# Two edge components in one 64-column matmul, in both layers of a graph network, and a reordered prologue

## The chip, the cores and the metric

The kernel runs on one core of a Trainium2 chip. The metric is the device time of one execution in microseconds (us), taken as the median over a number of runs. The engines are called PE (TensorE matmuls; PEld is its weight loads), DVE (VectorE), ACT (ScalarE), POOL (GpSimd) and SP (SyncE, which here issues DMAs).

## The reference

Two layers of an equivariant graph network follow each other, each as `x = layernorm(x + layer(x))`. There are 6,250 nodes and 200,000 edges, sorted by destination. A node has 64 scalars and 32 vectors of three components, 160 numbers in all. A layer does this:

```
h     = node_linear(x)                      # scalars 64x64, vectors 32x32, times a node attribute
w     = silu(edge_scalars @ W1) @ W2        # 10 -> 100 -> 192 in layer 1, 64 -> 64 -> 224 in layer 2
e0,e1 = edge_attr[:, :1], edge_attr[:, 1:4] # one scalar and one 3-vector for each edge
mid   = products of w, h[src] and e0/e1     # scalar, dot, outer, vector (layer 2: also the cross product)
agg   = segment_sum(mid, dst) / 4           # sum over the edges that end at a node
out   = self part of x + node_linear(agg)   # layer 2 ends with silu and sigmoid gates
```

## The kernel before, in words

**Edges.** 200,000 edges are 1,563 tiles of 128. Four tiles are a unit, so a layer has 391 units; two tiles are a pair. Consecutive tiles form groups of 3 to 12 (284 groups), such that the destinations of a group fit a window of 32 nodes. A check at run time (`flag`) makes sure of that; with other data a general branch (`general`) would run, which does not run here.

**A unit of a layer** (function `windows`) is spread over a software pipeline written by hand: `gather` (four units ahead) fetches the rows `h[src]` from DRAM with indirect DMAs on POOL, two per pair; `hidden` (three ahead) is the first edge matmul with its silu on ACT; `weights` and, on DVE, `places` and `products` are two ahead. `places` makes for each tile four matrices of 128 edges by 32 window positions: one-hot rows times the edge attribute component c = 0..3 (tile `sel`). `products` makes `mid`, the products of weights and gathered rows, in four instructions a pair in layer 1 and six in layer 2. `aggregate` then sums the edges of a tile on PE:

```python
for c, (at, step, k) in enumerate(sums):
    ...
    matmul(pg[32 * c:32 * c + 32, :k * V], s[:n, t % 2, c, :], o,
           start=first, stop=last, tile_position=(0, 32 * c))
```

That is four matmuls a tile, one for each edge component. Each has 32 weight columns at its own place of the array (0, 32, 64, 96) and writes its own 32 partitions of the accumulator `pg`. It streams k x 32 columns of `mid`: 5, 3, 3 and 3 blocks in layer 1, and 5, 5, 5, 5 in layer 2. PE's instructions are kept in program order.

**End of a group.** ACT copies `pg` to `r` (in layer 2 also the last 32 columns, block by block, to `rest`: L772). One unit later, `turn` transposes `r` on PE, and DVE adds it at the group's window into the node sums `sm` (four blocks) and `sr` (L788, L790).

**Nodes.** When a block of 128 nodes has all its edges, `second_nodes` or `last_nodes` multiplies its sums by the output weights (`rm0`, `rr0`, `rm1`, `rr1`), adds the self part and normalises; these steps are slipped in between units, one at a time.

**Prologue.** All node blocks are loaded, transposed (`turn_nodes`) and multiplied (`send_nodes`), and the result is stored to DRAM for the gathers, four blocks at a time and the short last block at the end. After the sixth of these steps DVE runs the check (`check`: 11 subtractions over 128 x 1,563 numbers, three reductions). After the last store, the products of layer 1's output weights are formed on PE and copied by DVE into `rm0` and `rr0` (L389 to L397), and the first gather follows.

The order across engines is that of the instructions in the program and of the buffers: eight buffers of gathered rows (`g`), three of weights (`pw`), six of `sel` and of `mid`, two of `pg`.

Of the kernel before, what the change touches and what calls it, by code (L numbers as in the profile page):

```python
# [86 lines left out]
def kernel(ctx: ExitStack, tc: tile.TileContext, a, out):  # L87
# [34 lines left out]
    SLOTS = (448, 640)  # L122
# [25 lines left out]
    chunks = [range(b, min(b + BG, NB - 1)) for b in range(0, NB - 1, BG)] + [range(NB - 1, NB)]  # L148
# [12 lines left out]
    def spread(t, s, v, n, q):  # L161

        nc.vector.memset(t, 0.0)
        q.dma_start(t[0:S, 0:n], a[s])
        for k in range(2):
            q.dma_start(t[S + k * V:S + k * V + V, n + k * V:n + k * V + V], a[v])
# [3 lines left out]
    spread(l1[:, 0], "Ws_l1_a", "Wv_l1_a", S, nc.scalar)  # L170
    spread(l1[:, 1], "Ws_l1_c", "Wv_l1_c", S, nc.scalar)
    ident = const.tile([P, P], F32, name="ident")
    make_identity(nc, ident)
    for j, (k, q) in enumerate((("a", nc.scalar), ("c", nc.gpsimd))):
        for r in range(0, P, V):
            q.dma_start(l1z[r:r + V, j, :], a[f"Wv_l1_{k}"])
# [47 lines left out]
    rm0 = const.tile([96, 4, 2, S + V], F32, name="rm0")  # L224
    rr0 = const.tile([64, 2, 2 * V], F32, name="rr0")
# [4 lines left out]

    limits = pre.tile([1, 2, NG], F32, name="limits")
    nc.gpsimd.memset(limits[:, 0], 0.0)
    for b, g in enumerate(READY):
        if g < NG:
            nc.gpsimd.memset(limits[:, 0, g:min(READY[b + 1], NG)], float(P * (b + 1)))
    g0 = 0
    while g0 < NG:
        g1 = g0
        while g1 < NG and zeroed(g1) == zeroed(g0):
            g1 += 1  # L240
        nc.gpsimd.memset(limits[:, 1, g0:g1], float(zeroed(g0) - W))
        g0 = g1

# [4 lines left out]
    def turn_nodes(bs, x):  # L248
# [12 lines left out]
        if (bs[0] // BG) % 2:  # L261
            nc.scalar.activation(xt[:, :w], p[:, :w], AF.Copy)
        else:
            nc.vector.tensor_copy(xt[:, :w], p[:, :w])
# [3 lines left out]
    def send_nodes(bs, xt, zt):  # L268
# [13 lines left out]
        for j, (b, q) in enumerate(zip(bs, qs)):  # L282
            t = rows[:n, j, :]
            nc.scalar.activation(t, q[:, 0, :], AF.Copy, scale=nv[:n, b, 0:1])
            nc.vector.scalar_tensor_tensor(t, q[:, 1, :], nv[:n, b, 1:2], t,
                                           op0=OP.mult, op1=OP.add)
# [14 lines left out]

    def check():

        basef = pre.tile([1, NG], F32, name="basef")
        nc.vector.tensor_copy(basef, base)
        nc.vector.tensor_copy(off, raw)
        p = psum.tile([P, 512], F32, name="pw", bufs=3)
        matmul(p[:, :NG], ones, basef, start=True, stop=True)
        for g0, g1 in segments:
# [3 lines left out]
            nc.vector.tensor_tensor(o, o, p[:, g0:g1, None].to_broadcast([P, m, n]), OP.subtract)  # L313

        nc.vector.memset(off[tail_e:, NT - 1:], 0.0)
        ends = pre.tile([P, 2], F32, name="ends")
        nc.vector.tensor_reduce(ends[:, 0:1], off, AX.X, OP.max)
        nc.vector.tensor_reduce(ends[:, 1:2], off, AX.X, OP.min)

        nc.vector.tensor_scalar(ends[:, 0:1], ends[:, 0:1], float(W - 1), None, op0=OP.subtract)  # L320
        nc.vector.scalar_tensor_tensor(over, ends[:, 1:2], -1.0, ends[:, 0:1],
                                       op0=OP.mult, op1=OP.max)

        nc.vector.tensor_tensor(limits[:, 0], limits[:, 0], basef, OP.subtract)
        nc.vector.tensor_tensor(limits[:, 1], basef, limits[:, 1], OP.subtract)
        nc.vector.tensor_reduce(tops[:, 1:2], limits, AX.XY, OP.max)

    def checked():
# [7 lines left out]
    previous = None  # L336
    for c, (bs, x) in enumerate(zip(chunks, xs)):
# [4 lines left out]
        if c == 5:  # L342
            check()
    send_nodes(previous[0], *previous[1])
    checked()


# [27 lines left out]

    p = psum.tile([P, 512], F32, name="pw", bufs=3)
    q = p[:96, :192].rearrange("p (j d) -> p j d", j=2)

    for j in range(2):
        for o, w, m in ((q[:, j, 0:S], w23[:, j * 96:j * 96 + 96], w23[:, 192:256]),
                        (q[:, j, S:], w23[:, 256 + j * 96:352 + j * 96], w23[:, 448:480])):
            matmul(o, w, m, start=True, stop=True)
        for k in range(2):
            matmul(p[k * V:k * V + V, 192 + j * V:224 + j * V],
                   w23[:, 320 + j * 96:352 + j * 96], w23[:, 448:480], start=True, stop=True,
                   tile_position=(0, k * V))
    nc.vector.tensor_copy(rm0[0:64, 0, :, 0:S], q[0:64, :, 0:S])  # L389
    nc.vector.tensor_copy(rm0[64:96, 0, :, S:], q[64:96, :, S:])  # L390

    for c, at_c, at_d in ((1, (32, 64), 0), (2, (0, 64), 32), (3, (0, 32), 64)):
        for k, r in enumerate(at_c):
            nc.vector.tensor_copy(rm0[r:r + 32, c, :, S:], q[32 * k:32 * k + 32, :, S:])
        nc.vector.tensor_copy(rm0[at_d:at_d + 32, c, :, 0:S], q[64:96, :, 0:S])
    for k in range(2):
        nc.vector.tensor_copy(  # L397
            rr0[k * V:k * V + V, :, k * V:k * V + V],
            p[k * V:k * V + V, 192:256].rearrange("p (j d) -> p j d", j=2))

# [6 lines left out]
    for at, n, f in ((0, 160, 0.125), (160, 32, r3 / 8), (192, 32, r2 / 8)):  # L407
# [8 lines left out]
            ((C0, vx), (F, vz), (C1, vx), (Dd, ss), (F, vy)),  # L416
            ((F, vz), (C0, vy), (C1, vy), (F, vx), (Dd, ss)),
            ((F, vy), (Dd, ss), (C0, vz), (F, vx), (C1, vz)))
# [7 lines left out]
    for o, f in ((rm1[:, :, 0:96], fs), (rm1[:, :, 96:], fv), (rr1[:, 0:96], fs),  # L426
                 (rr1[:, 96:], fv), (rm1[32:64, 1, vz], -1.0), (rm1[96:128, 2, vx], -1.0),
                 (rm1[0:32, 3, vy], -1.0)):
# [47 lines left out]
    def second_nodes(b, work, clear, name="nx"):  # L476
# [26 lines left out]
        def summed():  # L503
            p = psum.tile([P, 512], F32, name=bank[0], bufs=bank[1])
            q = p[:n, :2 * D].rearrange("p (w d) -> p w d", w=2)
            for c in range(4):
                l = sm[:96, c, rows]
# [6 lines left out]
            matmul(q[:, :, S + V:D], sr[:64, rows], rr0, start=False, stop=True)  # L514
# [25 lines left out]
    def last_nodes(b, work, clear):  # L540
# [19 lines left out]
        def summed():  # L560
# [5 lines left out]
            for c in (1, 2, 3):  # L566
                v = slice(96 if c == 2 else 0, 192)
# [26 lines left out]
    def windows(i, loads, work, inputs_of):  # L594
# [4 lines left out]
        scalar = lambda w, place: (w, V, 0, 2, place, 2)  # L599
        vector = lambda w, place, step, c=0, n=3: (w, 0, S + c * V, n, place, step)  # L600
        kinds = ((scalar(0, 2), scalar(S, 5), vector(128, 9, 2), vector(160, 0, 3)),
                 (scalar(0, 2), scalar(S, 10), vector(128, 9, 2), vector(160, 5, 3, 0, 2),
                  vector(160, 1, 1, 2, 1), vector(192, 0, 3)))[i]

        sums = (((5, 2, 5), (0, 2, 3), (2, 1, 3), (2, 2, 3)),
                ((9, 1, 5), (2, 1, 5), (0, 2, 5), (0, 1, 5)))[i]
# [144 lines left out]
        def aggregate(t):  # L751
# [6 lines left out]
            for c, (at, step, k) in enumerate(sums):  # L758
                o = mid[:n, t % 2, V * at:V * at + V]
                o = bass.AP(tensor=o.tensor, offset=o.offset, ap=[o.ap[0], [V * step, k], [1, V]])  # L760
                matmul(pg[32 * c:32 * c + 32, :k * V], s[:n, t % 2, c, :], o,
                       start=first, stop=last, tile_position=(0, 32 * c))
            if last:
                r = work.tile([P, 160], F32, name="r")
                w = (96, P)[i]
                nc.scalar.activation(r[:, :w], pg[:, :w], AF.Copy)  # L766
                if i == 0:
                    nc.scalar.activation(r[:32, 96:], pg[:32, 96:160], AF.Copy)
                else:
                    for c in range(4):  # L770
                        k = slice(32 * c, 32 * c + 32)
                        nc.scalar.activation(rest[g % 3][k, k], pg[k, P:P + V], AF.Copy)  # L772
                made["r", g] = r

        def turn(g):
            r = made["r", g]
            pt = pair[g % 2][:, 2 * P:]
            if i == 0:
                transpose(pt[:96, :P], r[:, :96], ident)
# [277 lines left out]
```

## Time and profile before

| what | value |
|---|---|
| median of 16 runs | 5844.52 us (5809.98 to 5873.43) |
| the profiled execution: time, span | 5881.2 us, 5879.4 us |
| mean granted TensorE clock | 0.758 |
| PE, DVE, POOL, ACT busy | 75%, 52%, 52%, 20% |
| first gather, first layer's last node step, end | 66.6 us, about 2945 us, 5879.4 us |

The profile is one execution. A line of it names the program's line, the engine, the operation and its tiles, written as result<-operands, with the number of instructions after an x. A group line goes on with busy time, the mean of one in ns, the idle time of the engine ahead of it, and what ended that. In a timeline line the first two numbers are the start and the length in us, and brackets hold idle time ahead of it with its releaser; "issue" means that the engine waited for nothing the profile shows. The clock row gives tenths of full TensorE speed. All matmuls of the main loop stand under L138, the line of a helper, and all transposes under L143, so tiles tell them apart: `pair<-e,fc` is `hidden`, `pw<-fc,h` is `weights`, `pg<-mid,sel` is `aggregate`, `pair<-ident,r` is `turn`, `pn` are node blocks.

### The profile page before, as it was taken

How to read it: one execution, taken by the hardware profiler on the slowest of the kernel's cores; microseconds unless marked ns; L12 is line 12 of the kernel's file. 1: busy time of each engine (PE TensorE's matmuls, PEld its weight loads, DVE VectorE, ACT ScalarE, POOL GpSimd, SP SyncE). 2: the span in 40 equal slices, each digit the busy share in tenths (PEclk: the TensorE clock that was granted, in tenths of full speed). 3: DMA queues.
4: the chain of work that ended last, by engine and by line, in shares of the span. 5: the costliest groups of instructions: out<-in, count | busy, mean ns of one | idle time of the engine just before them, and what ended most of it. 6: DMA issues, size and time to landing. Idle time of an engine off the chain costs nothing. (4 is left out here: it accounts for less than half of the span.)

```text
span 5879.4 us, 108061 instructions
## 1 busy us (share of the span) xinstructions
PE 4401.6 (75%) x37363; PEld 2847.1 (48%) x37363; DVE 3053.5 (52%) x13202; ACT 1172.6 (20%) x4012; POOL 3078.7 (52%) x3232
## 2 busy tenths in 40 slices
PE   7888877777777767777766777776777776677777
PEld 4555555555555545555534444444444444444554
DVE  5554444444445445444545555555555555555555
ACT  2111111111122212222211011111121222222333
POOL 4555555555555555554355555555555555544543
PEclk7787777777778777777767777777777777777777
DMA  3222222222222222222222222222222222222221
GB/s 101 59 62 58 59 55 56 55 53 56 55 55 55 54 55 56 53 55 53 52 65 67 68 69 69 70 68 68 68 69 66 68 66 65 66 62 65 67 66 44
DMA packets 298518, 364.06 MB, mean 62 GB/s; under 512 B 86324, under 2 KB 246205, under 8 KB 297965
## 3 DMA queue, kind: packets, MB, share of 16 engines
q0 software_dynamic: 151056, 257.36, 18.1%
q1 hardware_dynamic: 121740, 85.59, 5.6%
q10 hardware_dynamic: 25168, 14.11, 0.8%
q8 instruction: 301, 4.93, 0.3%
q14 instruction: 253, 2.06, 0.1%
HBM read 338.73 MB, written 18.03 MB: 61 GB/s over the span
## 5 line engine op out<-in xcount | busy, mean ns | idle before, releaser
L710 POOL DMA_INDIRECT g<-table,src x3126 | 3057.0, 978 | 2760.5 <-DVE mid L728 1538.2
L728 DVE TENSOR_TENSOR mid<-g,pw 128x128 f32<-128x128 f32 (+2 forms) x7820 | 1842.4, 298 | 458.1 <-remote 246.9
L138 PE MATMUL pg<-mid,sel 128*32 128x160 f32 (+1 forms) x25008 | 1600.1, 350 | 284.7 <-issue 281.3
L138 PE MATMUL pw<-fc,h 100*128 100x192 f32 (+1 forms) x6252 | 1463.1, 428 | 248.3 <-issue 189.6
L138 PEld LDWEIGHTS pw<-fc,h 100*128 100x128 f32 (+1 forms) x6252 | 1029.0, 231 | 734.0 <-issue 657.5
L138 PEld LDWEIGHTS pg<-mid,sel 128*32 128x32 f32 x25008 | 938.7, 132 | 685.0 <-issue 544.4
L741 DVE SCALAR_TENSOR_TENSOR sel<-iota,off,ea 128x128 f32<-128x128 f32 x3126 | 947.6, 341 | 594.2 <-remote 289.5
L788 DVE TENSOR_TENSOR sm<-pair,sm 96x128 f32 (+1 forms) x568 | 164.2, 289 | 1229.7 <-PE pair L143 386.2
L143 PE MATMUL pair<-ident,r 128*96 128x128 f32 (+1 forms) x852 | 262.9, 334 | 716.9 <-ACT h L672 339.1
L138 PE MATMUL pair<-e,fc 64*100 64x256 f32 (+1 forms) x2348 | 719.8, 517 | 59.7 <-issue 35.5
L143 PEld LDWEIGHTS pair<-ident,r 128*96 128x96 f32 (+1 forms) x852 | 124.6, 146 | 939.5 <-ACT h L672 373.4
L766 ACT ACTIVATE r<-pg 128x96 f32<-128x96 f32 (+1 forms) x568 | 149.3, 263 | 1917.1 <-remote 862.0
L138 PEld LDWEIGHTS pair<-e,fc 64*100 64x100 f32 (+1 forms) x2348 | 298.6, 212 | 302.6 <-issue 249.9
L672 ACT ACTIVATE h<-pair 100x256 f32<-100x256 f32 x782 | 259.0, 378 | 907.6 <-PE pair L138 324.3
L683 ACT ACTIVATE h<-pair 128x256 f32<-128x256 f32 x392 | 149.9, 383 | 961.9 <-remote 427.1
L138 PE MATMUL pn<-rm,sm 96*128 96x128 f32 (+3 forms) x968 | 193.7, 352 | 29.0 <-issue 26.0
L772 ACT ACTIVATE rest<-pg 32x32 f32<-32x32 f32 x1136 | 209.1, 184 | 12.6 <-issue 0.3
L138 PEld LDWEIGHTS pn<-rm,sm 96*128 96x128 f32 (+2 forms) x968 | 175.6, 234 | 46.6 <-issue 42.1
L138 PEld LDWEIGHTS pair<-fold,rest 128*128 128x128 f32 x568 | 132.6, 285 | 12.0 <-ACT rest L772 9.3
L143 PE MATMUL pn<-ident,nx 128*128 128x128 f32 (+1 forms) x242 | 66.6, 368 | 87.3 <-DVE nx L460 71.0
L517 DVE SCALAR_TENSOR_TENSOR nx<-pn,gets,nx 128x160 f32<-128x160 f32 x96 | 36.5, 380 | 171.8 <-PE pn L138 63.6
L440 ACT ACTIVATE xt<-pn 128x128 f32<-128x128 f32 (+1 forms) x146 | 40.4, 277 | 425.0 <-PE pw L138 200.8
(153 smaller groups left out, 1558.3 us busy)
## 6 DMA issues: line engine op xcount, KB each, us to landing
g<-table,src POOLq DMA_INDIRECT x3126
e<-in_e SPq DMA_DIRECT2D x781, 64.0 KB
e<-in_e SPq DMA_DIRECT2D x390, 20.0 KB
ea<-in_ea_main SPq DMA_DIRECT2D x63, 96.0 KB
xg<-in_x_main SPq DMA_DIRECT2D x12, 320.0 KB
table<-rg SPq DMA_DIRECT2D x12, 320.0 KB
xmid<-nx ACTq DMA_DIRECT2D x48, 80.0 KB
table<-nr ACTq DMA_DIRECT2D x48, 80.0 KB
```

The costliest lines, as they stand in the source:

```text
L138: r = nc.tensor.matmul(*args, **kw)
L143: r = nc.tensor.transpose(*args)
L440: nc.scalar.activation(xt[:, 0, :n], p[:, 0:n], AF.Copy)
L517: nc.vector.scalar_tensor_tensor(y, q[:, k, :], gets[:n, b, k:k + 1], y, op0=OP.mult, op1=OP.add)
L672: nc.scalar.activation(h[:100, 2 * P * j:2 * P * j + m], pair[j][:100, :m], AF.Silu)
L683: nc.scalar.activation(h[:kk, c0:c1], p[:kk, c0:c1], AF.Silu, scale=0.125)
L710: nc.gpsimd.indirect_dma_start(out=g[:n, j, :], out_offset=None, in_=table[i][:, :], in_offset=bass.IndirectOffsetOnAxis(ap=of(t)[0], axis=0))
L728: nc.vector.tensor_tensor(parts(mid[:n, :m], V * place, V * step, k), parts(g[:n, :m], c, V, k), parts(q[:n, :m], w, w_step, k), OP.mult)
L741: made["last"] = nc.vector.scalar_tensor_tensor(s[:n, j], iota[:n, None, :].to_broadcast([n, 4, W]), w, e[:, :, None].to_broadcast([n, 4, ...
L766: nc.scalar.activation(r[:, :w], pg[:, :w], AF.Copy)
L772: nc.scalar.activation(rest[g % 3][k, k], pg[k, P:P + V], AF.Copy)
L788: nc.vector.tensor_tensor(sm[:h, :, at], pt[:h, :P].rearrange("p (c w) -> p c w", c=4), sm[:h, :, at], OP.add)
```

## The change

A tile is aggregated with three matmuls instead of four: two of 32 weight columns and one of 64, which sums two edge components at once into 64 partitions.

- Layer 1: component 0 in 32 columns streams 5 blocks (160 columns), component 1 streams 4 blocks (128), components 2 and 3 together in 64 columns stream 4 blocks (128).
- Layer 2: component 0 and component 3 in 32 columns stream 5 blocks each (160), components 1 and 2 together in 64 columns stream 7 blocks (224).

A 64-column matmul gives both components all the blocks that either needs, so `mid` is laid out anew (`kinds`) and some sums are formed that are not used. In layer 1 the window sums now fill 128 partitions of `sm` and 32 of `sr`; the weights `rm0`, `rr0`, `rm1` and `rr1` follow, and a node block of layer 1 gets one more matmul. In layer 2 the end of a group has two more copies, since the used columns differ between partitions.

In the prologue the short block goes first. The check's conversions and subtractions move from DVE to POOL, its three reductions stay on DVE, each placed behind a block's last sum. The composed weights are formed in the middle, copied once by ACT, and placed by DVE three copies at a time. Eight DMAs that repeated a small weight become two. The general branch is adapted to the new layout.

```diff
-        sums = (((5, 2, 5), (0, 2, 3), (2, 1, 3), (2, 2, 3)),
-                ((9, 1, 5), (2, 1, 5), (0, 2, 5), (0, 1, 5)))[i]
+        sums = (((0, 1, 5, 1, 5), (1, 1, 0, 1, 4), (2, 2, 1, 1, 4)),
+                ((0, 1, 9, 1, 5), (3, 1, 0, 1, 5), (1, 2, 1, 1, 7)))[i]
...
-            for c, (at, step, k) in enumerate(sums):
+            for c, m, at, step, k in sums:
+                q = c if i == 0 else (0, 2, 3, 1)[c]
...
-                matmul(pg[32 * c:32 * c + 32, :k * V], s[:n, t % 2, c, :], o,
-                       start=first, stop=last, tile_position=(0, 32 * c))
+                matmul(pg[32 * q:32 * (q + m), :k * V],
+                       s[:n, t % 2, c:c + m, :].rearrange("p c w -> p (c w)"), o,
+                       start=first, stop=last, tile_position=(0, 32 * q))
...
-                    for c in range(4):
+                    nc.scalar.activation(r[64:96, :P], pg[64:96, V:V + P], AF.Copy)
+                    nc.scalar.activation(
+                        r[96:, :P].rearrange("p (h v) -> p h v", h=2),
+                        pg[96:, :192].rearrange("p (h v) -> p h v", h=2)[:, :, :2 * V], AF.Copy)
+                    for c, at in enumerate((P, P, P + V, P + 2 * V)):
...
-            matmul(q[:, :, S + V:D], sr[:64, rows], rr0, start=False, stop=True)
+            matmul(q[:, :, S + V:S + 2 * V], sm[:, 0, rows], rr0[:, 0], start=False, stop=False)
+            matmul(q[:, :, S + 2 * V:D], sr[:V, rows], rr0[:V, 1], start=False, stop=True)
...
-    chunks = [range(b, min(b + BG, NB - 1)) for b in range(0, NB - 1, BG)] + [range(NB - 1, NB)]
+    chunks = [range(NB - 1, NB)] + [range(b, min(b + BG, NB - 1)) for b in range(0, NB - 1, BG)]
...
-            nc.vector.tensor_tensor(o, o, p[:, g0:g1, None].to_broadcast([P, m, n]), OP.subtract)
+            nc.gpsimd.tensor_tensor(o, o, base_of[:, g0:g1, None].to_broadcast([P, m, n]),
+                                    OP.subtract)
...
+        if c == 3:
+            nc.gpsimd.tensor_copy(basef, base)
+            nc.gpsimd.tensor_copy(off, raw)
+        if c == 6:
+            bases()
+            check()
+        if c == 7:
+            small = composed()
+        if c > 7:
+            for step in small[:3]:
+                step()
+            small = small[3:]
+        if c > 8 and reduces:
+            with tc.issue_after(last[0].ins):
+                reduces.pop(0)()
```

## The prediction

> **What bounds the kernel now.** I read the page first: the span, the busy shares and the granted clock.
>
> ```profile
> span 5879.4 us, 108061 instructions
> ...
> PE 4401.6 (75%) x37363; PEld 2847.1 (48%) x37363; DVE 3053.5 (52%) x13202; ACT 1172.6 (20%) x4012; POOL 3078.7 (52%) x3232
> ...
> PEclk7787777777778777777767777777777777777777
> ```
>
> PE is the busiest engine, at a mean granted clock of 0.76. The busy time cut into prologue with first fill, layer 1 and layer 2 says how much slack each has:
>
> ```profile
> 105.00:2945.00 2840.00, 2209.72 (x18949) 1496.62 (x18948) 1398.91 (x5790) 540.76 (x1726) 1509.08 (x1537) 0.77 0.23 56
> 2945.00:5879.00 2934.00, 2123.91 (x18054) 1302.37 (x18054) 1596.89 (x7203) 604.94 (x2207) 1522.29 (x1563) 0.74 0.27 66
> ```
>
> Columns: window, its length, busy PE, PEld, DVE, ACT, POOL, then clock. PE idles 630 us in layer 1 and 810 us in layer 2; DVE and POOL are near half. What ends PE's idle time, from its waits:
>
> ```profile
> PE pair L143 <- ACT h L672: 339.1, 99, 7.3
> PE pair L143 <- ACT h L683: 291.5, 64, 8.7
> PE pg L138 <- issue: 281.3, 493, 2.5
> PE pw L138 <- issue: 189.6, 341, 2.4
> ```
>
> With the smaller rows, 578 us are "issue" (PE waits for nobody that the profile shows) and some 860 us are the rest, mostly the group's transpose waiting behind ACT. So PE's own work is most of a unit of four tiles, and the waits come on top. Then the timeline, around single bursts of the aggregation. First the weight loads, then PE:
>
> ```profile
> 1508.80 0.95 PEld L138 LDWEIGHTS pg<-mid,sel 128*32 128x32 f32 x32 [0.23 <-issue]
> 1510.00 0.31 PEld L138 LDWEIGHTS pair<-e,fc 64*100 64x100 f32 x3 [0.25 <-issue]
> ...
> 4420.96 0.97 PEld L138 LDWEIGHTS pg<-mid,sel 128*32 128x32 f32 x32
> 4422.18 0.30 PEld L138 LDWEIGHTS pair<-e,fc 128*128 128x128 f32 x2 [0.25 <-issue]
> ...
> 4443.75 1.80 PEld L138 LDWEIGHTS pg<-mid,sel 128*32 128x32 f32 x32
> 4446.04 0.50 PEld L138 LDWEIGHTS pair<-e,fc 128*128 128x128 f32 x2 [0.49 <-issue]
> ...
> 4010.52 0.73 PEld L138 LDWEIGHTS pg<-mid,sel 128*32 128x32 f32 x16
> 4011.74 0.50 PEld L138 LDWEIGHTS pair<-e,fc 128*128 128x128 f32 x2 [0.49 <-issue]
> ```
>
> ```profile
> 4000.26 0.75 PE L138 MATMUL pg<-mid,sel 128*32 128x160 f32 x16
> 4000.94 0.70 PE L138 MATMUL pair<-e,fc 128*128 128x256 f32 x2
> ```
>
> Each matmul leaves two records (two passes), so a unit's 16 matmuls are 32, and a round is one pass in each of the four places. Three readings. (1) A unit's burst takes 1.20 us in layer 1 (1508.80 to 1510.00) and 1.22 us in layer 2 (4420.96 to 4422.18), although layer 1 streams 160+96+96+96 columns a tile and layer 2 four times 160. The four places run side by side, and the widest, 160 in both layers, sets the time. (2) Eight rounds take 1.22 us and four 0.68 (4000.26 to 4000.94): a round costs 0.135 us and a burst 0.14 us once. At half clock (windows on these bursts give a clock of 1.00 and 0.50) it is 2.29 and 1.22: 0.267 and 0.15. (3) The once-only part sits at the change of shape: the weight loader idles 0.25 us (0.49 at half clock) before the first load of another shape, waiting for nobody, while its 32 loads of one shape have no such gap.
>
> **The change, part by part.**
>
> *Three matmuls a tile.* The built program has, per tile, 32 columns, 32 columns, 64 columns, then the next tile's 32: two changes of shape a tile. The trace shows many pairs of shapes among ordinary matmuls (rows 32, 64 or 128 against columns 32 or 128), and each has the gap; 32 against 64 columns at unlike places is not among them. Bounds: below, no gap, the three side by side; above, the gap each time. I take the upper one, because the gap comes with every pair of shapes that occurs, also where only rows or only columns differ.
>
> Then a tile is two bursts. The 32-column pair: two rounds at 160, 2 x 0.135 + 0.14 = 0.41 us. The 64-column one in layer 1: 128 columns, 2 x 0.108 + 0.14 = 0.36; in layer 2: 224 columns, 2 x 0.189 + 0.14 = 0.52. A unit: 4 x 0.77 = 3.06 us in layer 1 and 4 x 0.93 = 3.71 in layer 2, against 1.22: +1.84 and +2.49. At half clock 5.05 and 6.34 against 2.29: +2.76 and +4.05. The clock rows 0.77 and 0.74 mean 46% and 52% of the time at half speed: +2.26 and +3.30 a unit, times 391 units: 884 + 1290 = 2174 us of PE work.
>
> What hides it: PE's waits for others. They come as 99 waits of 3.4 us and 64 of 4.6 us; a unit that is 2.26 or 3.30 us longer swallows about 69% of each, of 860 us some 595. The issue gaps stay; matmul and weight-load records fall by 12,504 of 74,726, 17%, so I take 17% of 578 off: 98 us. Net 2174 - 595 - 98 = +1481. Bounds: all at full clock with every wait swallowed, (1.84 + 2.49) x 391 - 860 = +830; all at half clock with nothing swallowed +2660.
>
> [...]
>
> *Copies after a group.* Layer 2 gets two more ACT copies, 568 in all at 184 to 276 ns: 105 to 157 us of an engine that is 20% busy. PE reads them a unit later, so the unit hides them: 0, and at most 157 if not. Layer 1's copy goes from 250 to 276 ns: 0. DVE's sums over 96 or 128 partitions are 288 and 290 ns, its products keep their number: 0.
>
> *Node blocks.* One more matmul in each of 49 blocks: two records of 376 ns become two of about 282 (row 96x64) and two of about 355 (row 32x64), +0.5 us each, 0 to +25; taken +13.
>
> *Prologue.* The work before the edges ends on DVE:
>
> ```profile
> 66.62 1.04 POOL L710 DMA_INDIRECT g<-table,src  x1 [40.51 <-DVE rr L397]
> ...
> 38.54 1.22 PE L138 MATMUL pg<-l,xt 128*128 128x256 f32 x2 [6.07 <-DVE rg L285]
> ```
>
> The check held PE for 6.07 us, and the copies into rm and rr from 62.82 to 66.1 stand between the last store and the first gather. Both go: -9.4. Against it: the short block's load goes ahead on SP (0.66 us) and the last block sent is now a full one (about 1 us): -8. Queued on POOL instead: 11 subtractions of 1,563 columns. No POOL row shows such an operation; its memset of 768 columns took 0.76 us, its select of 128 took 0.33, so 1.6 to 4 us. POOL idles 40.5 us there and nothing else is queued behind but the gathers, which wait for DVE anyway; without that cover, +4. Eight l1z loads become two, ahead of nothing late: 0. The fallback branch is not run: 0.
>
> Sum: 1481 + 13 - 8 = +1486 on the profiled 5881 us, 7367; the median of the runs lies 37 us under that execution: **7330 us**.
>
> **Rivals.**
>
> *Side by side after all, slower by the widest* (16%). 32 and 64 columns overlap without a gap. Layer 1 keeps 160 as its widest and pays nothing; layer 2 goes to 224: a round 0.054 us longer, 0.107 at half clock, 0.65 a unit, 255 us, less 64 waits x 0.65 = 42, less 98 of issue, less 8: +107, so 5951. For it: the places are independent within one shape. Against: reading (3).
>
> *Faster through fewer instructions* (15%). As before, but layer 2's wider place is never last, because the unit's end is set by ACT's transposes and issue gaps. Then only -98 and -8 remain: 5738. It decides if layer 2's units are not longer by even 0.27 us on average, the point where 0.27 x 391 = 106 us uses the gain up. For it: the timeline's units vary from 3 to 14 us, so other things than the burst decide many. Against: no idle on PE long enough in most units.
>
> *No change to measure* (5%): the two cancel. That the change is not what it says is ruled out by the built program.
>
> **How the numbers follow.** The gap case has 64%: seen at every change of shape, unseen at this one. Its own range is 6750 to 8050, inside its bounds of 6674 and 8504. The rivals lie at 5951 and 5738. A range from 5780 to 8000 leaves out most of the faster case (12%) and the top of the gap case (7%). About 0.3% (18 us) is what a measurement of this kernel can tell from no change; faster by more has 15%, within 5%, slower by more 64 + 16 = 80%.
>
> **What would show it.** In the changed profile: bursts of pg with a unit at 3 to 6 us instead of 1.2 to 2.3; weight loads of 128x64 starting over 0.2 us after the matmul before them; PE busy over 85% and POOL's wait for DVE mid longer; the first gather near 58 us. A unit's burst near 1.2 us in layer 1 and 1.6 in layer 2, at full clock, would make the gap wrong; more than 17% less issue idle would favour the faster case. A granted clock far from 0.76 would move the size, not the sign.

## The result, and the profile after

The changed kernel takes 6068.97 us in the median (6046 to 6107), the kernel before 5849.37 us beside it: a ratio of 1.0385, 95% interval [1.0363, 1.0407]. The sign of the forecast holds and the time lies inside its range, but the size is wrong: +220 us came where +1486 were worked out. The profiled execution took 6054.6 us.

The page of the changed kernel, the rows that answer to those of before:

```profile
span 6052.8 us, 95930 instructions
...
PE 5297.5 (88%) x31205; PEld 2752.8 (45%) x31205; DVE 3048.8 (50%) x13185; ACT 1364.2 (23%) x4583; POOL 3128.1 (52%) x3248
...
PEclk8898898888897898888788898998999989989898
```

PE's busy time grew by 896 us and the span by 173 (the profiled execution of before was slower than its median, that of the changed kernel faster). The clock row, sevens before, is eights and nines: 0.879 in the mean instead of 0.758. By stage, with the same columns as before (layer 2 begins near 3000 us):

```profile
105.00:3000.00 2895.00, 2655.97 (x15935) 1505.86 (x15933) 1394.70 (x5784) 546.16 (x1730) 1528.33 (x1536) 0.86 0.22 54
3000.00:6052.00 3052.00, 2573.86 (x14912) 1200.34 (x14912) 1597.06 (x7203) 790.42 (x2770) 1542.71 (x1563) 0.90 0.25 63
```

PE idles 239 us in layer 1 (630 before) and 478 in layer 2 (810). Its waits:

```profile
PE pair L143 <- ACT h L712: 299.6, 97, 7.4
PE pair L143 <- ACT h L701: 144.2, 71, 5.6
...
PE pg L138 <- issue: 60.8, 104, 3.2
...
PE pw L138 <- issue: 14.9, 22, 2.2
```

The waits of the group's transposes for ACT's `h` fell from 631 to 444 us. The idle time at `pg` and `pw` that was put down to "issue" fell from 471 to 76. Now the timeline around two bursts in layer 2, weight loads of one first, then PE of the other (granted clock 1.00 in both):

```profile
4557.24 0.19 PEld L138 LDWEIGHTS pg<-mid,sel 128*64 128x64 f32 x2 [0.25 <-issue]
4557.76 0.14 PEld L138 LDWEIGHTS pg<-mid,sel 128*32 128x32 f32 x4 [0.33 <-issue]
4558.16 0.19 PEld L138 LDWEIGHTS pg<-mid,sel 128*64 128x64 f32 x2 [0.25 <-issue]
```

```profile
4580.53 3.74 PE L138 MATMUL pg<-mid,sel 128*32 128x160 f32 x24
```

The gap that the forecast assumed is there at every change between 32 and 64 columns inside the bursts (5270 in the trace, the weight loader idle for 0.12 us at the least, 0.25 or 0.33 us in the median, by direction), and a unit's burst in layer 2 at full clock takes 3.67 us until the next matmul starts (4580.53 to 4584.20; forecast 3.71). So the price of the edit was read rightly. What shrank is elsewhere. The groups of PE, before and then after (busy time, mean ns, idle time ahead):

```profile
L138 PE MATMUL pg<-mid,sel 128*32 128x160 f32 (+1 forms) x25008 | 1600.1, 350 | 284.7 <-issue 281.3 <-DVE mid L728 1.1
L138 PE MATMUL pw<-fc,h 100*128 100x192 f32 (+1 forms) x6252 | 1463.1, 428 | 248.3 <-issue 189.6 <-DVE mid L728 52.1 <-PE pw L138 0.9
```

```profile
L138 PE MATMUL pg<-mid,sel 128*32 128x160 f32 x18756 | 3065.4, 347 | 62.6 <-issue 60.8 <-PE pg L138 0.4
L138 PE MATMUL pw<-fc,h 100*128 100x192 f32 (+1 forms) x6252 | 1136.8, 377 | 27.3 <-issue 14.9 <-DVE mid L757 11.0 <-ACT h L712 0.5
```

`pw` was not touched by the edit, and yet it is 326 us shorter.

### The profile page after: what moved, and what is told of

Read it like the earlier page. It is cut to its first block, busy times and chain, and to the rows that moved or that the text cites. A ratio compares the mean times of both kernels' runs of the same rounds, so it can differ in the third digit from the quotient of the medians.

```text
span 6052.8 us, 95930 instructions
## 1 busy us (share of the span) xinstructions
PE 5297.5 (88%) x31205; PEld 2752.8 (45%) x31205; DVE 3048.8 (50%) x13185; ACT 1364.2 (23%) x4583; POOL 3128.1 (52%) x3248
## 4 chain that ended last, share of the span: by engine, by line
PE 71%; another core or an unknown queue 12%; ACT 7%; issue 5%; DVE 3%; ACTq 0%; DMA 0%; DVEq 0%; SPq 0%
PE pg L138 42%; PE pw L138 13%; PE pair L138 7%; PE pn L138 5%; PE pair L143 3%; ACT rest L808 2%; DVE mid L757 2%; ACT h L712 1%; PE pn L143 1%; ACT r L797 1%; ACT h L701 1%; ACT r L802 1%; DVE sel L770 1%; ACT r L803 0%
## 5 line engine op out<-in xcount | busy, mean ns | idle before, releaser
L739 POOL DMA_INDIRECT g<-table,src x3126 | 3098.8, 991 | 2854.1 <-DVE mid L757 1649.7
L138 PE MATMUL pg<-mid,sel 128*32 128x160 f32 x18756 | 3065.4, 347 | 62.6 <-issue 60.8
L138 PEld LDWEIGHTS pg<-mid,sel 128*32 128x32 f32 x18756 | 1143.0, 125 | 1769.7 <-issue 1733.7
L138 PE MATMUL pw<-fc,h 100*128 100x192 f32 (+1 forms) x6252 | 1136.8, 377 | 27.3 <-issue 14.9
L138 PEld LDWEIGHTS pw<-fc,h 100*128 100x128 f32 (+1 forms) x6252 | 854.4, 201 | 335.6 <-issue 302.7
L823 DVE TENSOR_TENSOR sm<-pair,sm 128x128 f32 x568 | 165.4, 291 | 1463.1 <-PE pair L143 475.5
L143 PE MATMUL pair<-ident,r 128*128 128x128 f32 x852 | 233.8, 300 | 560.4 <-ACT h L712 299.6
L797 ACT ACTIVATE r<-pg 128x128 f32<-128x128 f32 x568 | 157.3, 277 | 2003.6 <-PE pg L138 1184.6
L138 PE MATMUL pair<-e,fc 64*100 64x256 f32 (+1 forms) x2348 | 578.1, 453 | 17.9 <-DMA e<-in_e 7.1
L138 PE MATMUL pn<-rm,sm 128*128 128x128 f32 (+3 forms) x968 | 153.5, 309 | 0.4 <-issue 0.4
L138 PEld LDWEIGHTS pn<-rm,sm 128*128 128x128 f32 (+1 forms) x968 | 146.4, 204 | 11.1 <-issue 8.3
```

What stands on the lines that cost most here:

```text
L138: r = nc.tensor.matmul(*args, **kw)
L143: r = nc.tensor.transpose(*args)
L739: nc.gpsimd.indirect_dma_start(out=g[:n, j, :], out_offset=None, in_=table[i][:, :], in_offset=bass.IndirectOffsetOnAxis(ap=of(t)[0], axis=0))
L797: nc.scalar.activation(r[:, :P], pg[:, :P], AF.Copy)
L823: nc.vector.tensor_tensor(sm[:, :, at], pt[:, :P].rearrange("p (c w) -> p c w", c=4), sm[:, :, at], OP.add)
```

## Experiments

Theory: the gap at a change of shape costs what was forecast, but the granted clock answers to how busy PE is, so added PE work is partly paid back by everything else that PE does. Rivals: layer 2's 224 columns or the copies carry the cost; PE's bursts are not on the path at all.

The runs took place on several chips, and each ratio compares kernels on one chip. Two kinds of chip showed up: on one (called slow; also that of the first comparison) the kernel before takes 5834 to 5916 us, on the other (quick) 4101 to 4108 us. Each chip was used in one stretch of time only, so that the chip itself makes the difference is not shown.

| kernel | slow: ratio, interval, clock | quick: ratio, interval, clock |
|---|---|---|
| before | 1, clock 0.758 | 1, clock 0.901 |
| changed | 1.0385 [1.0363, 1.0407], 0.879 | 1.1963 [1.1932, 1.1993], 0.981 |
| changed, no change of shape | 1.0019 [0.9992, 1.0046] and 1.0061 [1.0038, 1.0084], 0.79 | not run |
| changed, bursts grouped | 0.9948 [0.9927, 0.9968], 0.874 | 1.0741 [1.0721, 1.0762], 0.978 |
| before, streams x2 | 1.0157 [1.0121, 1.0193], 0.857 | not run |
| before, streams x3 | 1.0203 [1.0169, 1.0237], 0.925 | 1.1675 [1.1647, 1.1703], 0.993 |
| before, narrow streams | 1.0013 [0.9991, 1.0035], 0.641 | 1.0151 [1.0109, 1.0193], 0.733 |

**Without the changes of shape** (slow kind, twice).

```diff
-                matmul(pg[32 * q:32 * (q + m), :k * V],
-                       s[:n, t % 2, c:c + m, :].rearrange("p c w -> p (c w)"), o,
-                       start=first, stop=last, tile_position=(0, 32 * q))
+                for j in range(m):
+                    matmul(pg[32 * (q + j):32 * (q + j) + 32, :k * V], s[:n, t % 2, c + j, :], o,
+                           start=first, stop=last, tile_position=(0, 32 * (q + j)))
```

> The changed kernel with each 64-column matmul written as two of 32 columns at neighbouring places, same operands, same streams (layer 1: 160, 128, 128, 128 columns a tile; layer 2: 160, 160, 224, 224). No change of shape inside a unit's burst is left; the 224 columns, the two more copies a group, the new node layout and the new prologue stay. Theory A (the gap at every change of shape is what the 220 us are): a unit's burst goes back to 1.22 us in layer 1 and 8 x 0.189 + 0.14 = 1.65 us in layer 2 at full clock, the granted clock falls back to about 0.76, and the time lies between 5840 and 5950 us, with layer 1 as long as before. Rival B (the wider stream of layer 2, the copies or the new layout carry the time): it stays within 60 us of the changed kernel's 6069 us and layer 2 keeps its length of about 3100 us.

> The changed kernel with each 64-column matmul written as two of 32 columns, once more. On the quick kind, theory A (the changes of shape are the cost): burst 1.22 us in layer 1 as before, 1.65 us in layer 2 at full clock, +0.43 us on a unit that gathers bound at 4.9 us: ratio 0.99 to 1.03, clock 0.91 to 0.94. Rival B (the wider stream, the copies or the layout): ratio above 1.10. On the slow kind: 0.999 to 1.005 again.

Measured 1.0019 and 1.0061, at a clock of 0.79 where 0.76 was expected. Nearly all of the 3.85% goes with the changes of shape; the 224 columns, two more copies a group, the new layout and the new prologue together cost 0.2 to 0.6%. The rival of the wider stream falls for the slow kind; on the quick kind this kernel was not run.

**Same instructions, fewer changes of shape** (slow, then quick).

```diff
+                if wide != (m == 2):
+                    continue
...
-                for t in range(4 * u, min(4 * u + 4, NT)):
...
-                    aggregate(t)
...
+                for wide in (False, True):
+                    for t in range(4 * u, min(4 * u + 4, NT)):
...
+                        aggregate(t, wide)
```

> The changed kernel, but of a unit's four tiles all 32-column matmuls are issued first and then all 64-column ones: same instructions, 2 bursts a unit in place of 8. Theory A: the burst costs 1.22 us + (8 x 0.108 + 0.14) = 2.22 us in layer 1 and 1.22 + 1.65 = 2.87 us in layer 2 at full clock, against 3.06 and 3.71; six of the eight 0.14-us drains go, 0.84 us a unit at full clock. If the time follows the added PE work in proportion, 40% of the 220 us go: about 5980 us (5930 to 6020), with a granted clock between 0.79 and 0.86. Rival B (the wider stream or the copies): no change from 6069 us. Rival C (what counts is how long the last tile of a group takes until its copy): slower than 6069, since every group now closes at the end of its unit.

> The changed kernel with a unit's 32-column matmuls before its 64-column ones, once more. Slow kind of chip: ratio 0.993 to 0.997 again. Fast kind, theory S: PE's own unit is 0.84 us shorter than with the gaps, 4.3 to 4.5 us, below POOL's 4.9, so the ratio is 0.98 to 1.02. Rival (PE's added work in full): 1.00 + 1.65 us a unit, +1040 us, ratio 1.25.

The weight loads of a unit (layer 1, slow chip) show one gap for each of two bursts:

```profile
1400.42 0.95 PEld L138 LDWEIGHTS pg<-mid,sel 128*32 128x32 f32 x16 [0.23 <-issue]
1401.63 0.85 PEld L138 LDWEIGHTS pg<-mid,sel 128*64 128x64 f32 x8 [0.25 <-issue]
```

The bursts start 1.21 us apart, as forecast (1.22). On the slow kind the kernel is even faster than before (0.9948, 5808 us), a bigger step than the 5930 to 6020 us expected. On the quick kind it is 7.4% slower where at most 2% was expected: PE is busy about 95% of the span there (its seven largest waits add up to 186 of 4409 us), and that expectation had taken the shortest unit for the mean one, without the node blocks.

**The same PE work without any change of shape** (slow, then quick). In the kernel before, every matmul streams its columns three times (and, in another run, twice); the repeats go to unused columns.

```diff
-                o = bass.AP(tensor=o.tensor, offset=o.offset, ap=[o.ap[0], [V * step, k], [1, V]])
-                matmul(pg[32 * c:32 * c + 32, :k * V], s[:n, t % 2, c, :], o,
+                o = bass.AP(tensor=o.tensor, offset=o.offset,
+                            ap=[o.ap[0], [0, 3], [V * step, k], [1, V]])
+                matmul(pg[32 * c:32 * c + 32, :3 * k * V], s[:n, t % 2, c, :], o,
```

> The kernel before, its four 32-column matmuls a tile unchanged in number and shape, but each streams its columns three times over (480 columns in place of 160; the first 160 carry the result, the rest goes to unused columns of the same accumulator). No change of shape is added. A unit's burst is 24 rounds of 0.135 us + 0.14 = 3.38 us at full clock, as much as the changed kernel's mean of 3.06 and 3.71. Theory A1 (any work of PE in that place costs the same, and the granted clock rises because PE is busier or the kernel slower): clock about 0.88 and a time of 6000 to 6150 us. Theory A2 (the granted clock answers to what the array streams, and the gaps at changes of shape are rest to it, so that after's bursts were paid back by a faster clock): the clock is not above 0.76, the added 2.16 us a unit at full clock and 4.3 at half come out near +3.2 us a unit, 2500 us of PE work, of which PE's idle time hides some 700: a time of 7300 to 8300 us.

> The kernel before with every 32-column matmul streaming its columns twice (320 in place of 160, the second time into unused columns). A unit's burst is 16 x 0.135 + 0.14 = 2.30 us at full clock against 1.22; times 782 units +845 us at full clock, +1670 at half. Theory (a busier PE holds the full clock for longer, and that pays most of the added work back; the threefold stream came out at clock 0.925 and +113 us): clock near 0.85, time between 5800 and 5900 us. Rival (the clock of the threefold stream was something else, PE's work adds at the old mix of clocks): clock 0.76 and 6300 us or more.

> The kernel before with every 32-column matmul streaming its columns three times over, once more. On the quick kind, theory S (PE's own work sets the unit, whatever it consists of): as the changed kernel, whose bursts are as long (3.06 and 3.71 against 3.38 us), ratio 1.16 to 1.20 at a clock near 0.98. Rival (the changes of shape cost more than their bursts show, by weight loads that come late for the next matmuls): ratio below 1.12. On the slow kind: 1.017 to 1.024 again.

The page of the threefold stream on the slow kind:

```profile
PE 5210.8 (88%) x37363; PEld 2427.2 (41%) x37363; DVE 3133.5 (53%) x13202; ACT 1175.8 (20%) x4012; POOL 3014.2 (51%) x3232
...
PEclk8999999999999999999989988898899899999999
```

and its `pg` group:

```profile
L138 PE MATMUL pg<-mid,sel 128*32 128x480 f32 (+1 forms) x25008 | 3073.4, 555 | 54.4 <-issue 49.3
```

PE's `pg` work, 3073 us, is that of the changed kernel (3065), and it costs 2.0% in place of 3.85%. The rest of PE's work is 2137 us here and 2232 in the changed kernel, at clocks of 0.925 and 0.879; why the clock is lower beside the gaps was not asked. Theory A2, a clock not above 0.76 and 7300 us or more, fails; theory A1 had the direction, but 5953 us lies under its 6000 to 6150 and the clock over its 0.88. The twofold stream came out at 1.0157 (6001 us, beside 5916 on that chip), more than expected, with its clock in between (0.857). On the quick kind the threefold stream costs 16.75%, as theory S had it, beside the changed kernel's 19.6%. By layer, the longer burst has the longer time: between first gathers, layer 1 takes 2473 us with the threefold stream and 2394 with the change (bursts of 3.38 and 3.06 us), layer 2 takes 2255 and 2451 (3.38 and 3.71). There, gaps and plain streaming of the same length cost about the same.

**Less PE work** (slow, then quick; most of the sums are left out). In the kernel before, one block of 32 columns is streamed after a group's first tile.

```diff
                 o = mid[:n, t % 2, V * at:V * at + V]
+                if not first:
+                    k = 1
```

> The kernel before, but after the first tile of a group every matmul of the aggregation streams one block of 32 columns in place of three or five (most of the sums are left out of the result; instructions and their order stay). A unit's burst falls from 1.22 us to some 0.5 to 0.7 us at full clock. Theory (the clock follows how busy PE is, and gives back in both directions): some 500 us of PE work less at full clock, the clock falls below 0.74, and the time stays within 1.5% of before, 5760 to 5900 us. Rival (PE's work sets the time in proportion, at a fixed clock): 5843 less about 600, near 5300 us.

> The kernel before with one block of 32 columns in place of three or five after the first tile of a group, once more (most of the sums are left out). On the quick kind, theory S: the gathers on POOL, 4.9 us a unit, stay, so at best 3950 us, ratio 0.96 to 1.00, with a clock below 0.88. Rival (PE's work is on the path there too): ratio below 0.93. On the slow kind: 0.999 to 1.004 again, clock 0.64.

Groups of PE on the slow kind, and the clock row:

```profile
L138 PE MATMUL pw<-fc,h 100*128 100x192 f32 (+1 forms) x6252 | 1722.8, 502 | 192.4 <-issue 96.6 <-DVE mid L728 81.0 <-DVE mv L457 10.3
L138 PE MATMUL pg<-mid,sel 128*32 128x32 f32 (+2 forms) x25008 | 891.6, 263 | 458.4 <-issue 454.8 <-PE pg L138 1.5
...
PEclk7666666556666665665566666666666666656666
```

`pg` lost 709 us and `pw`, untouched, gained 260; the time did not move (1.0013). On the quick kind less work even made the kernel 1.5% slower, at a clock of 0.733 against 0.901; the expected gain (a ratio of 0.96 to 1.00) did not come. Only the length of the streams differs between these kernels, so that the clock follows PE's work, in both directions, is shown: a clock of 0.641, 0.758, 0.857, 0.925 on the slow kind for a narrow, single, double and threefold stream.

**The quick kind by itself.** The kernel before and the changed kernel there (rows of the page, and the group of `pg`):

> The kernel before, for its profile on this chip. On a chip of the quick kind: span near 4100 us, clock 0.90, no stretches of 0.7 us an instruction on PE, a unit of 5.1 us on average and PE busy 85 to 90%. On the slow kind: 5820 to 5920 us as in the first profile.

> The changed kernel once more, beside the kernel before on the same chip. Two kinds of chip have been seen: on two of them the kernel before takes 5840 and 5916 us, on a third 4101 us, where PE's stretches of 0.7 us an instruction and the waits for an unknown releaser are gone and a unit takes 5.1 us, close to POOL's own 4.9 us of gathers. On the slow kind: ratio 1.03 to 1.05 again. On the fast kind, theory S (without those stalls a unit is as long as its busiest engine): PE's own unit with three matmuls is 5.1 to 5.3 us where nothing waits, above POOL's 4.9, so 4200 to 4450 us, ratio 1.03 to 1.08. Rival (on the fast kind PE's added work is on the path in full, as the prediction had it): 391 x (1.84 + 2.49) = 1690 us at full clock, 5500 us or more, ratio above 1.3.

```profile
span 4100.0 us, 108061 instructions
...
PE 3497.8 (85%) x37363; PEld 2403.6 (59%) x37363; DVE 3060.7 (75%) x13202; ACT 1182.0 (29%) x4012; POOL 3028.9 (74%) x3232
...
PEclk8898998898999999899888898888898999999998
...
L138 PE MATMUL pg<-mid,sel 128*32 128x160 f32 (+1 forms) x25008 | 1170.2, 308 | 0.0
```

```profile
span 4910.2 us, 95930 instructions
...
PE 4748.2 (97%) x31205; PEld 2547.9 (52%) x31205; DVE 3040.9 (62%) x13185; ACT 1367.9 (28%) x4583; POOL 3109.9 (63%) x3248
...
PEclk8999999999999999998999999999999999989999
...
L138 PE MATMUL pg<-mid,sel 128*32 128x160 f32 x18756 | 2710.2, 318 | 0.0
```

The change costs 804 us there. Theory S said 4200 to 4450 us, and 4910 came; its idea holds (PE is the busiest engine and fills 97% of the span, which also answers, for this kind, the rival that PE's bursts are not on the path), its number again took the shortest units (5.1 and 5.3 us) for the mean (6.1 and 6.2 us in the two layers). The rival with all of the added work on the path, 5500 us, fails too. What the quick kind lacks shows in ACT's waits, the kernel before on the slow and then on the quick kind:

```profile
ACT r L766 <- remote: 862.0, 120, 11.6
...
ACT h L683 <- remote: 427.1, 50, 11.4
...
ACT h L672 <- remote: 317.2, 76, 12.3
```

```profile
ACT r L766 <- PE pg L138: 1023.4, 496, 6.6
ACT h L672 <- PE pair L138: 540.8, 346, 10.1
ACT h L683 <- PE pair L138: 520.9, 168, 8.6
```

"remote" is a releaser that the profile does not know: 1606 us of waiting in these three rows on the slow kind, none on the quick. With them goes a second sign: records of PE (matmuls and weight loads) that start 0.64 to 0.76 us behind the one before and wait for no semaphore are counted 616 times in the trace of before on the slow kind, 77 times in the changed kernel there, and once and never on the quick kind. On the slow kind there are 375 in the threefold stream, 511 without the changes of shape and 150 with the bursts grouped, so longer streams alone make them fewer; whether fewer matmuls do so too was not told apart.

Three more runs, also on the quick kind, asked what else sets the time; the expectations of the first two rest on the slow kind's numbers.

```diff
-            for j in range(2):
+            for j in range(1):
```

That is the gather; the products of a pair's second tile read the first tile's rows.

> The kernel before with one indirect gather a pair in place of two; both tiles of a pair multiply the same gathered rows (half of the gathered data is left out of the result). POOL's gathers fall from four to two a unit: 4 x (978 + 253 ns) = 4.9 us to 2.5 us; PE, DVE and ACT instructions stay. The run with the narrow streams had shown that some 700 us less of PE work bring nothing. Theory P (gathers set the pace behind everything, so PE's work was never the bound): the time falls by 300 us or more, below 5600 us, and the granted clock rises. Theory Q (the pace is set by the chain from PE over ACT and DVE back to PE, at a clock that answers to it): within 1% of before.

3500.1 against 4100.7 us, 0.8527 [0.8501, 0.8552]: on the quick kind the gathers set the pace of the kernel before, as theory P had it. POOL's time in gathers (3007 us before, 1681 here) and the data they moved (257.4 and 129.3 MB) both fall by about half, so which of the two it is stays open.

```diff
-            for w, w_step, c, k, place, step in kinds:
+            for w, w_step, c, k, place, step in kinds + kinds[:2]:
```

> The kernel before with the first two products of every pair made twice (same operands, same result), so that DVE has four more instructions of about 0.3 us in each unit: 782 x 4 x 0.3 = 930 us, busy share from 52% to 66%. Theory D (DVE lies in the chain that sets a unit): the time rises by 400 to 900 us. Theory Q' (DVE waits for others anyway and hides it): less than 1% up. If the time rises, the granted clock falls below 0.75, since PE idles more.

4252.1 us, 1.0367 [1.0341, 1.0393]: between the two theories. The added products are 609 us of DVE work (2454.8 against 1846.1), of which a quarter reaches the end; the clock fell from 0.90 to 0.882, the way that was expected.

> The kernel before with every 32-column matmul of the aggregation written as two, each over half of its columns: the same streams, 25,008 more matmul and as many more weight-load records (74,726 to 124,742). On the slow kind, theory I (the stalls come with the number of PE instructions that have to be brought): blocks of 256 instructions go from 301 to about 490, which came every 19 us, so the time goes up by 20% or more, far beyond the +1.6% of the twofold stream, and stretches of 0.7 us an instruction multiply. Rival (the stalls have nothing to do with their number): ratio 1.00 to 1.04. On the quick kind: ratio 1.00 to 1.12, by the weight loads, without stalls.

```diff
+                for b, m in ((0, (k + 1) // 2), ((k + 1) // 2, k // 2)):
...
+                    matmul(pg[32 * c:32 * c + 32, V * b:V * (b + m)], s[:n, t % 2, c, :], x,
...
```

It ran on the quick kind: 0.9998 [0.9980, 1.0017]. 25,008 more matmul records cost nothing there. The blocks of 256 are an estimate from the instruction queue: 301 packets in the trace of before and 253 in that of the changed kernel, which has 12,316 fewer PE records, 257 for a packet. On the slow kind it was not tried, so whether the stalls there come with the number of PE instructions stays open.

**Parts that might win.** The changed prologue alone, in the kernel before (slow kind, twice; its diff is that of the change):

> The changed prologue alone (short block first, check on POOL, output weights formed and copied early); the four matmuls a tile, the products, the copies and the node layout are those of before. Theory: the first gather comes 8 us earlier and nothing else moves: about 5840 us against 5849, a ratio near 0.9986, at the edge of what can be told. Rival: the moved work delays the prologue elsewhere or the gain is swallowed by the first fill: ratio 1.000 or above.

> The changed prologue alone, once more. Theory: the first gather some 2 us earlier in the profile (64.45 against 66.62 us in the first runs) and nothing else: ratio 0.996 to 1.000 on the quick kind, 0.995 to 0.999 on the slow kind. Rival: the 16 us that it gained in the first run came from elsewhere, and the ratio scatters around 1.

0.9973 [0.9954, 0.9992] and 0.9982 [0.9960, 1.0004], 10 to 16 us; the second is not clear of no change. In the profiles the first gather came 2.2 and 2.1 us earlier (64.45 and 64.52 for 66.62), so most of the small gain has no place that these runs show.

The grouped bursts in layer 1 alone (slow, then quick). Against the grouped kernel, layer 2 has its four matmuls, products, copies and output weights of before again:

```diff
-                for wide in (False, True):
+                for wide in (False, True)[:2 - i]:
```

> The changed prologue; in layer 1 the changed aggregation with a unit's 32-column matmuls first and its 64-column ones after; in layer 2 the four matmuls a tile, products, copies and layout of before. The grouped run had layer 1 at 2778 us against 2884 before and 2856 with the changed prologue alone, and layer 2 at 2978 against 2929 and 2906. Theory (the two layers stand by themselves, and layer 2 loses by its 224-column stream while layer 1 gains): layer 1 near 2780, layer 2 near 2915, time 5740 to 5790 us, ratio 0.982 to 0.991. Rival (the layers' lengths in single profiles scatter by 1%, and there is nothing to win by mixing): as the grouped run, 5790 to 5830 us.

> Layer 1 with the grouped three matmuls, layer 2 as before, the changed prologue, once more. Slow kind of chip: ratio 0.980 to 0.987 again. Fast kind, theory S: both layers stay under POOL's gathers, ratio 0.985 to 1.01; the gain of the slow kind, which came with fewer PE instructions and fewer stalls, is gone.

0.9832 [0.9797, 0.9868] on the slow kind, the best of all there, and 1.0171 [1.0154, 1.0189] on the quick kind, past the 0.985 to 1.01 expected. No version that touches the aggregation beat the kernel before on both kinds.

## Why the prediction was right and wrong

| us | forecast | measured, slow | measured, quick |
|---|---|---|---|
| PE work of `pg` | +2174 | +1465 | +1540 |
| PE's other work | +13 | -569 | -290 |
| PE idle (waits and issue) | -693 | -722 | -440 |
| prologue | -8 | within the rest | within the rest |
| span | +1486 | +173 | +810 |

The measured rows are differences of the pages: busy time of the `pg` group, the rest of PE's busy time, and span less busy time.

**Right: the price of the edit.** Take the forecast's own unit prices (3.06 and 5.05 us in layer 1, 3.71 and 6.34 in layer 2, at full and half clock) and put in the clock that the changed kernel had, 0.858 and 0.897 between the first gathers of the layers and the end (28% and 21% of the time at half): 3.62 + 4.25 = 7.88 us, times 391 is 3080 us of `pg`. Measured: 3065. On the quick kind, at 0.98, the same sum gives 2714; measured 2710. The two forecast bounds for 32 against 64 columns, no gap or the full gap, are decided for the gap (5270 changes, each with at least 0.12 us). What PE does in it, which an expectation above calls a drain, no run shows. The reason that the forecast gave, a gap at every pair of shapes, does not hold: three of its own rows (`pg` at 4420.96, 4443.75 and 4010.52 us) follow loads of 128x128 and 32x128 without one. In that the right choice had some luck.

**Right in the sum, by luck: what PE's idle time swallows**, 693 forecast and 722 measured. Its two parts are both off. The waits for others gave some 290 us where 595 were forecast (the transposes' for ACT's `h` 187), and issue gave 428 (at `pg` and `pw` 395), where 98 were taken in proportion to the instructions. By the forecast's own test ("more than 17% less issue idle would favour the faster case") this would speak for the rival "faster through fewer instructions". But the threefold stream, with no fewer instructions, cut issue from 578 to 221 us as well, so their number is not shown to be the reason.

**Wrong: the step "the clock rows 0.77 and 0.74 mean 46% and 52% of the time at half speed".** It is a reading of the kernel before, and it was used as the price list of a kernel that keeps PE busier. The clock went to 0.879. At the old mix the prices give 391 x (3.97 + 5.08) = 3540 us for the changed bursts, 460 more than at the new one. And all other PE work became 569 us shorter, a term that the sum did not have at all; scaled by the mean clock alone, 2801 x (1 - 0.758/0.879) = 386 us of it. In the clock records 1341 us of that work ran at half clock before and 442 after. So by this estimate 846 of the missing 1313 us are the clock. Another 235 us come from the base: the kernel before measures 1600 us of `pg` where the prices give 1365; on the quick kind they give 1120 against 1170, so the stalls of the slow kind probably stand in it, which no run separated. The other 183 us of the 569 stay open; the stalls can hardly be all of them, since on the quick kind, without stalls, the same estimate leaves 100 of 290 us too (2328 x (1 - 0.901/0.981) = 190). The forecast's own sentence, that another clock would move the size and not the sign, was true, but neither the middle nor the range was worked out for it.

**Luck: the range.** That the time lies in the stated range is luck. The range reaches down to 5780 us for the rivals' sake, and the time lies 600 us under the gap case's own lower bound, 6674 us, which took the full clock for the bursts of both kernels and repriced nothing else.

The clock records of these two traces know two levels, 0.5 and 1.0, in pieces of 3.41 us or multiples of it, but for one piece in each (311 pieces of each level before, 157 after; the median piece is 6.83 us before and 17.07 after). What moves the clock from one level to the other was not shown. Shown is that the mean rises with the length of the streams (0.641 for the narrow to 0.925 for the threefold stream), and the forecast had no term for it.

**The rest.** The gap case was the right one, and "side by side after all" and "faster through fewer instructions" are decided against by the bursts of the changed kernel (3.67 us a unit where side by side would give about 1.6) and by the kernel without changes of shape: the same 224 columns cost 0.2 to 0.6%, and the two more copies are inside that, so their price of 0 was near enough. PE busy over 85%, weight loads over 0.2 us late and a longer wait of POOL for `mid` (1538.2 to 1649.7 us) came as announced. The first gather did not: forecast near 58 us, it came at 64.09 us. The check and the copies that were taken out had stood beside something else: the last store of node rows is issued at 62.50 us before and 60.37 after, and the first gather follows it by 4.1 and 3.7 us in both. That store was probably what the first gather waited for next, and it was not asked for. Node blocks could not show their +13 us under a faster clock (`pn<-rm,sm` fell from 193.7 to 153.5 us).

## What to carry to other kernels

A granted clock below 1 is not a constant of the machine (0.758 became 0.879 here): price a change of PE work at the clock that the changed kernel will have, and remember that every other matmul is repriced with it (`pw`, untouched, went from 1463 to 1137 us), so that a PE that waits often gives much of the added work back (+1465 us of `pg` became +173 us of span) and work taken away may bring nothing (709 us less of `pg`, a ratio of 1.0013). Matmuls of 32 and of 64 weight columns did not run side by side here, and each change between them cost about 0.14 us at full clock (an estimate: the 3.67 us of a unit's burst less 2.59 for its rounds, over eight) and a late weight load (by 0.25 or 0.33 us); if both shapes are needed, let each run in one long burst (1.0385 became 0.9948, 1.1963 became 1.0741). And measure on more than one chip before a ratio is trusted: here the same edit is +3.9% or +19.6%.

## What was not expected of the hardware

The same kernel takes 4101 to 4108 us on some chips and 5834 to 5916 on others. In the slow trace of before ACT waits 1606 us for "remote", and 616 records of PE start about 0.7 us behind the one before though they wait for nothing; the quick one has none of the first and one of the second. The changed kernel loses less by it: the slow kind adds 1744 us to the kernel before (5845 - 4101), 1159 to the changed one. The cause was not found.

And less work for PE can make a kernel slower: with most of the aggregation's columns left out, the quick kind went from 4108 to 4174 us, at a clock of 0.733 in place of 0.901.
